# Two order edges in a state-space scan: where the addition to Y and the product dt*x stand in VectorE's queue

## The chip, the cores and the metric

The kernel runs on one core of one Trainium2 chip. The metric is device microseconds of one execution; the figure compared is the median of several runs. In what follows PE is TensorE, DVE is VectorE, ACT is ScalarE, POOL is GpSimd and SP is SyncE, which here only issues DMAs.

## The reference, cut to what matters

Four layers are applied in turn to a float32 image batch of shape (8, 64, 64, 64). The first three (attention over a whole image, two blocks of window attention, a dynamic filter with a 1x9 convolution) run beside the change. The change lies in the fourth, which contains a selective scan in four directions. Per image there are K = 4 directions, DI = 128 channels, L = 4096 positions and N = 16 states:

```python
dts = softplus(einsum(dts, dtproj_w) + dtproj_b)          # dt per channel and position
A = -exp(A_logs)
h = h * exp(dt * A) + dt * B * u                           # for each of the 16 states
y = sum over the states of h * C                           # for each channel and position
out_y = y + D * u
...
y = out_y[:, 0] + inv[:, 0] + wh + invwh                   # the four directions are added
```

## The kernel before, in words

The eight images are taken as four pairs. While the fourth layer's scans of one pair run, the same instruction streams carry other work: the end of the pair before (`back`) and the first layers of the pair after (`front`: attention, window attention, filter, scan inputs). The function `scans` hands out both in small pieces, and a scheduler that builds the program then fixes one order for each engine. It places each instruction by its own estimates of when its inputs are ready, so an instruction may stand ahead of others that were handed out before it. The order edge `net.behind(a, b)` (L445) tells that scheduler to place `a` after `b`; it adds no semaphore.

The scans of a pair are cut into 64 units: two images, four directions in the order 1, 3, 0, 2, and eight pieces of 512 positions (`TD`). A unit has eight steps of two states each. With step number i counted through the pair, one turn of the loop in `scans` does this:

- `fetch` has SP issue the transfers that spread the B row of step i+3 and the C row of step i+2 over the partitions (L1759, 256 KB each, tiles `B` and `C`, four buffers each).
- `products` has POOL form v = B * (dt*x) for step i+2 (L1767, 128x1024, eight buffers).
- `step` does for each of its two states an exponential on ACT into a PSUM bank (L1789, tile `dad`), the scan on DVE (L1792), the copy of the scan's last column on ACT (L1800, tile `carry`), and the product with C on POOL or DVE (L1803, L1806).
- `sums` has PE add the products into the PSUM tile `yd` (L1818, four matmuls a step). `yd` has one buffer; a unit's first sum can start only when the unit before has been read out of it.
- Where i is 2 modulo 8, `gather` is called for the unit before: DVE adds `yd` to the accumulator `Y` (L1831 for the first direction, with D*x; L1833 for the next two; L1836 for the last, into the tile `xs`, which SP then stores).
- After steps 0, 1 and 2 of a unit come `load`, `inputs` and `spread` of the next unit. `inputs` computes dt: PE (L1730) into a PSUM bank, tile `pdd`, then ACT exponential, logarithm and copy (L1732, L1735, L1736); PE and ACT then make the B and C rows (L1738, L1740) and SP stores them (L1742). `spread` has DVE form dt*x from that bank (L1748; it and dt go into the tile `du1`, which has one buffer) and SP issue the two transfers that spread dt and dt*x from there over the partitions (L1752, 512 KB each, tile `du`).

`pdd`, `pbc` and `dad` share three PSUM banks (tag `da`); in the last pair the exponentials also use the three banks of the other work. A bank with dt in it is freed when dt*x has been formed.

In what follows the 16 scans of a unit are counted 0 to 15; step 2 has scans 4 and 5.

Of the kernel before, what the change touches and what calls it, by code (L numbers as in the profile page):

```python
# [11 lines left out]
ALU = mybir.AluOpType  # L12
# [226 lines left out]
class _Net:  # L239
    def __init__(self, ctx, tc, x, packs, layout, out):  # L240
        self.tc, self.nc = tc, tc.nc
        self.x, self.out = x, out
        nc = self.nc
        self.const = ctx.enter_context(tc.tile_pool(name="const", bufs=1))
        self.dram = ctx.enter_context(tc.tile_pool(name="rows", bufs=2, space=bass.MemoryType.DRAM))
        self.packs, self.layout, self.w = packs, layout, {}
        self.load(self.const, (0, 1))
        with tc.tile_pool(name="temp", bufs=1) as temp:
            self.load(temp, (2,))
            self.prepare()  # L250
# [910 lines left out]
class _Direct:  # L1161
# [8 lines left out]
    def __init__(self, net, ctx):  # L1170
        self.net, self.tc, self.nc, self.w = net, net.tc, net.nc, net.w
        tc = self.tc
        self.dram = ctx.enter_context(tc.tile_pool(name="mem", bufs=2, space=bass.MemoryType.DRAM))
        self.slabs = ctx.enter_context(tc.tile_pool(name="slabs", bufs=3))
        self.ps = ctx.enter_context(tc.tile_pool(name="ps_scan", bufs=3, space=PSUM))
        self.pf = ctx.enter_context(tc.tile_pool(name="ps_front", bufs=3, space=PSUM))
        self.kept = {}
        self.turn = -1
        self.dense = 0

    def begin(self, ctx):


        tc = self.tc
        with tc.tile_pool(name="slabs0", bufs=3) as slabs, tc.tile_pool(name="w00", bufs=2) as pool:
            ahead = _Apart(self, slabs, pool).first(1)
            front = first = done = 0
            for cost in self.front(0):
                front += cost
                if cost == 0:  # L1190
                    first = front
                while first and done < AHEAD * (front - first):
                    done += next(ahead, front)
            self.run(ahead)
        one = ctx.enter_context(tc.tile_pool(name="scan1", bufs=1))
        self.Y = one.tile([P, L], F32, name="Y", tag="Y")
        self.carries = one.tile([P, NST], F32, name="carry", tag="carry")
        self.sw = ctx.enter_context(tc.tile_pool(name="scan", bufs=2))
        return front, first
# [544 lines left out]
    def spread(self, u):  # L1744

        nc, one = self.nc, u["one"]
        du = u["du"] = self.sw.tile([P, GRP, 2, TD], F32, name="du", tag="du")
        nc.vector.tensor_tensor(one[:, 1], u["pd"], u["x"], ALU.mult)  # L1748
        m = P // GRP
        for g in range(GRP):  # L1750
            src = one[m * g : m * g + m].rearrange("c q t -> c (q t)").unsqueeze(1).to_broadcast([m, GRP, 2 * TD])
            nc.sync.dma_start(du[:, g].rearrange("p q t -> p (q t)"), src)  # L1752
# [16 lines left out]
    def step(self, i, st):  # L1769

        nc, w, net = self.nc, self.w, self.net
        wk, ps = self.sw, self.ps
        u = self.units[i // 8]
        k, c, at, CC, v = u["k"], u["c"], u["at"], st["C"], st["v"]


        n0 = 2 * (i % 8)
        own = 1 + (i % 4 == 3) if u["image"] >= B - 2 else i % 2 + self.dense
        rev = k >= 2

        def along(t):
            return t[:, ::-1] if rev else t

        h = wk.tile([P, 2 - i % 2, TD], F32, name="hd", tag=f"h{i % 2}", bufs=2)
        hs = []
        for j in range(2):
            n = n0 + j
            da = self.bank("dad", (P, TD), "da")
            nc.scalar.activation(da, u["du"][:, j, 0], AF.Exp, scale=net.As[:, k, n : n + 1])  # L1789
            first = 0.0 if at == 0 else self.carries[:, n : n + 1]  # L1790
            to = da if j >= 2 - own else h[:, j]
            nc.vector.tensor_tensor_scan(along(to), along(da), along(v[:, j]), first, ALU.mult, ALU.add)  # L1792
            hs.append(to)
            if at < NTD - 1 and (own or j):
                ends = h[:, :, 0] if rev else h[:, :, TD - 1]
                cs = self.carries[:, n0 : n0 + 2]
                if own:
                    ends = to[:, 0:1] if rev else to[:, TD - 1 : TD]
                    cs = self.carries[:, n : n + 1]
                nc.scalar.activation(cs, ends, AF.Copy)  # L1800

        if own == 0:
            st["w"] = nc.gpsimd.tensor_tensor(v, h, self.twice(CC), ALU.mult)  # L1803
        for j in range(2 if own else 0):
            engine = nc.vector if j >= 2 - own else nc.gpsimd
            m = engine.tensor_tensor(v[:, j], hs[j], CC, ALU.mult)  # L1806
            st.setdefault("w", m)
# [16 lines left out]
    def gather(self, u):  # L1824

        nc, net, k, c = self.nc, self.net, u["k"], u["c"]
        y = u["y"]
        yd = net.part(self.Y, k, c)
        yp = y.rearrange("p (a b) -> p a b", b=64)
        if u["nth"] == 0:  # L1830
            nc.vector.scalar_tensor_tensor(yd, self.img(u["x"]), net.dsum, yp, ALU.mult, ALU.add)  # L1831
        elif u["nth"] < 3:
            nc.vector.tensor_tensor(yd, yd, yp, ALU.add)  # L1833
        else:
            o = u["x"]
            nc.vector.tensor_tensor(self.img(o), yd, yp, ALU.add)  # L1836
            nc.sync.dma_start(u["out"][:, c * TD : (c + 1) * TD], o)


# [152 lines left out]
```

## Time and profile before

| | |
|---|---|
| median of 3 runs | 12877.57 us (12873.15 to 12906.72) |
| the profiled execution, its own time | 12896.13 us |
| its span in the trace | 12894.0 us |
| mean granted TensorE clock | 0.817 |
| busy: PE, DVE, POOL, ACT | 9714.9, 8570.4, 7760.9, 7066.2 us |
| DVE: L1831, L1833, L1836 (256 in all) | 70.5, 125.3, 43.7 us |
| DVE: L1748 (256) | 174.0 us |
| DVE: the scans L1792 (4096) | 2712.4 + 1782.6 + 363.5 + 248.9 us |

Busy time is the time in which an engine executes. Idle time ahead of an instruction is charged to the instruction that ended it. The first 2200 us of the span hold the first layers of pair 0, with the first layer of pair 1 beside them, and no scans; then the four pairs of scans run one after the other to the end.

### The profile page before, as it was taken

Reading aid. Unit: us, or ns where it says so; the run is one execution under the profiler, and the core shown is the slowest. Engines: PE = TensorE matmul, PEld = TensorE weight load, DVE = VectorE, ACT = ScalarE, POOL = GpSimd, SP = SyncE. Lnnn points to the kernel's source line nnn. Section 1 sums busy time; section 2 is a strip of 40 time slices with the busy share of each in tenths; the row PEclk is TensorE's granted clock in tenths of the full one; section 3 lists DMA queues with packets and bytes.
Section 4 is the critical chain, followed back from the end, with each engine's and each line's share of the span. In section 5 each row is a group of like instructions: output and inputs, shape, how many; then the busy total and the mean of one; then the engine's idle time right before and its main releaser. Section 6 shows DMA issues by size and latency. Waiting matters only on the chain. (4 is left out here: it accounts for less than half of the span.)

```text
span 12894.0 us, 141975 instructions
## 1 busy us (share of the span) xinstructions
PE 9714.9 (75%) x46358; PEld 3162.6 (25%) x46358; DVE 8570.4 (66%) x10061; ACT 7066.2 (55%) x15577; POOL 7760.9 (60%) x3875
## 2 busy tenths in 40 slices
PE   9999985788786558988888556997898655555556
PEld 2243421333221112224332111222342101111111
DVE  0121245788878785467776778358776778998888
ACT  5556523565646655655654645665654645455444
POOL 0000001999899883457765795347775698877774
PEclk9999976787787678988888667998888767777667
DMA  0000002555555552334443564234443456556553
GB/s 25 1 1 1 1 13 87 160 165 158 159 162 167 177 162 84 98 119 128 139 124 108 168 182 129 70 104 135 136 123 105 142 179 192 172 167 187 173 172 125
DMA packets 779985, 1579.99 MB, mean 123 GB/s; under 512 B 89312, under 2 KB 89440, under 8 KB 778208
## 3 DMA queue, kind: packets, MB, share of 16 engines
q1 hardware_dynamic: 755040, 1514.49, 38.5%
q10 hardware_dynamic: 24192, 56.32, 1.1%
q8 instruction: 367, 6.01, 0.2%
q14 instruction: 386, 3.16, 0.1%
HBM read 1199.26 MB, written 102.76 MB: 101 GB/s over the span
## 5 line engine op out<-in xcount | busy, mean ns | idle before, releaser
L1767 POOL TENSOR_TENSOR vd<-B,du 128x1024 f32<-128x1024 f32 x2048 | 4816.6, 2370 | 3728.7 <-DMA B<-rows 2391.2
L1818 PE MATMUL yd<-vd,pack 128*64 128x512 f32 x8192 | 3042.7, 782 | 1327.0 <-POOL vd L1806 648.1
L1789 ACT ACTIVATE dad<-du,As 128x512 f32<-128x512 f32 x4096 | 2734.4, 681 | 1236.0 <-DVE hd L1792 568.7
L1792 DVE TENSOR_TENSOR_SCAN hd<-dad,carry,vd 128x512 f32<-128x512 f32 x2166 | 2712.4, 1270 | 510.2 <-ACT dad L1789 295.7
L1803 POOL TENSOR_TENSOR vd<-hd,C 128x1024 f32<-128x1024 f32 x658 | 1557.8, 2367 | 648.4 <-DVE hd L1792 372.5
L1806 POOL TENSOR_TENSOR vd<-hd,C 128x512 f32<-128x512 f32 x1154 | 1484.4, 1291 | 614.9 <-DVE hd L1792 599.3
L1792 DVE TENSOR_TENSOR_SCAN dad<-dad,carry,vd 128x512 f32<-128x512 f32 x1418 | 1782.6, 1273 | 87.4 <-ACT dad L1789 87.2
L1320 ACT ACTIVATE e<-s 128x512 f32<-128x512 f32 x2048 | 1202.9, 592 | 835.4 <-PE s L1314 833.8
L1818 PEld LDWEIGHTS yd<-vd,pack 128*64 128x64 f32 x8192 | 657.3, 166 | 3329.1 <-POOL vd L1806 1120.2
L1314 PE MATMUL s<-X 64*128 64x512 f32 x4096 | 1302.2, 650 | 43.0 <-ACT e L1320 35.2
L1806 DVE TENSOR_TENSOR vd<-dad,C 128x512 f32<-128x512 f32 x1626 | 1081.4, 677 | 289.7 <-ACT carry L1800 269.0
L1306 PE MATMUL po<-e,VT 128*64 128x512 f32 x4096 | 1204.8, 625 | 7.4 <-ACT e L1320 7.2
L1800 ACT ACTIVATE carry<-hd 128x1 f32<-128x1 f32 (+1 forms) x1586 | 313.9, 201 | 741.1 <-DVE hd L1792 731.1
L1730 PE MATMUL pdd<-xs,xdt 128*128 128x512 f32 x512 | 406.0, 886 | 375.0 <-DVE hd L1792 168.7
L1472 PE MATMUL w_av<-vals,wide 64*64 64x9 f32 x16384 | 624.7, 213 | 36.4 <-ACT wide L1462 36.1
L1472 PEld LDWEIGHTS w_av<-vals,wide 64*64 64x64 f32 x16384 | 597.2, 155 | 216.7 <-issue 90.6
L1457 DVE TENSOR_TENSOR wide<-w_s,bias 128x512 f32<-128x512 f32 x512 | 329.3, 681 | 394.0 <-PE w_s L1444 389.5
L1800 ACT ACTIVATE carry<-dad 128x1 f32<-128x1 f32 x1422 | 239.0, 168 | 630.4 <-DVE dad L1792 626.3
L1314 PEld LDWEIGHTS s<-X 64*128 64x128 f32 x4096 | 355.4, 187 | 912.6 <-issue 794.3
L1329 DVE COPY att<-po 128x512 f32<-128x512 f32 x32 | 21.9, 686 | 755.9 <-PE po L1306 755.9
L1247 PE MATMUL pv<-n_sq,pack 128*128 128x512 f32 x576 | 355.8, 702 | 183.5 <-ACT n_sq L1245 175.8
L1833 DVE TENSOR_TENSOR Y<-Y,yd 128x512 f32<-128x512 f32 x128 | 125.3, 979 | 519.9 <-PE yd L1818 519.9
(246 smaller groups left out, 11236.7 us busy)
## 6 DMA issues: line engine op xcount, KB each, us to landing
B<-rows SPq DMA_DIRECT2D x2048, 256.0 KB, 3.6
C<-rows SPq DMA_DIRECT2D x2048, 256.0 KB, 3.4
du<-du SPq DMA_DIRECT2D x512, 512.0 KB, 6.1
xs<-xt SPq DMA_DIRECT2D x128, 256.0 KB, 3.7
xs<-xc SPq DMA_DIRECT2D x128, 256.0 KB, 3.8
xc<-xcv ACTq DMA_DIRECT2D x64, 256.0 KB, 2.1
zs<-z ACTq DMA_DIRECT2D x64, 256.0 KB, 3.5
xt<-XT ACTq DMA_DIRECT2D x32, 512.0 KB, 5.3
```

The costliest lines, as they stand in the source:

```text
L1306: nc.tensor.matmul(po[half[im]], lhsT=VT[:, t, half[im]], rhs=es[im], start=(t == 0), stop=(t == 31))
L1314: nc.tensor.matmul(ss[im], lhsT=at(half[im], t), rhs=X[half[im], jc * CH : (jc + 1) * CH], start=True, stop=True)
L1320: nc.scalar.activation(e, ss[im], AF.Exp, scale=C**-0.5, accum_out=parts[:, im, t, jc : jc + 1])
L1472: nc.tensor.matmul(self.av[half[im], x % 4 + j, h, :], lhsT=es[h // 4][half[im], j, h % 4, :], rhs=V[half[im], x + j, h, :], start=True, s ...
L1730: nc.tensor.matmul(pd, lhsT=net.xdt[:, k, :], rhs=x, start=True, stop=True)
L1767: self.nc.gpsimd.tensor_tensor(v, self.twice(st["B"]), self.units[i // 8]["du"][:, :, 1], ALU.mult)
L1789: nc.scalar.activation(da, u["du"][:, j, 0], AF.Exp, scale=net.As[:, k, n : n + 1])
L1792: nc.vector.tensor_tensor_scan(along(to), along(da), along(v[:, j]), first, ALU.mult, ALU.add)
L1800: nc.scalar.activation(cs, ends, AF.Copy)
L1803: st["w"] = nc.gpsimd.tensor_tensor(v, h, self.twice(CC), ALU.mult)
L1806: m = engine.tensor_tensor(v[:, j], hs[j], CC, ALU.mult)
L1818: m = nc.tensor.matmul(u["y"][self.HALF[j]], lhsT=w["fold"], rhs=st["v"][:, j], start=(i % 8 == 0), stop=(i % 8 == 7))
```

## The change

The class keeps the DVE scan that was issued last in `self.scanned`. Two order edges are added: the addition to `Y` in `gather`, and the product dt*x in `spread`, are placed behind that scan. Both are called after step 2 of a unit, so the scan is the second one of step 2, scan 5. The first dt*x of a pair stands behind the last scan of the pair before, and only the first of the whole run has no scan to stand behind. No instruction is added or taken away, and no semaphore is changed by hand; the scheduler builds all five queues anew.

```diff
     def spread(self, u):
...
-        nc.vector.tensor_tensor(one[:, 1], u["pd"], u["x"], ALU.mult)
+        m = nc.vector.tensor_tensor(one[:, 1], u["pd"], u["x"], ALU.mult)
+        if self.scanned is not None:
+            self.net.behind(m, self.scanned)
...
     def step(self, i, st):
...
-            nc.vector.tensor_tensor_scan(along(to), along(da), along(v[:, j]), first, ALU.mult, ALU.add)
+            self.scanned = nc.vector.tensor_tensor_scan(
+                along(to), along(da), along(v[:, j]), first, ALU.mult, ALU.add
+            )
...
     def gather(self, u):
...
+        o = u["x"]
         if u["nth"] == 0:
-            nc.vector.scalar_tensor_tensor(yd, self.img(u["x"]), net.dsum, yp, ALU.mult, ALU.add)
+            m = nc.vector.scalar_tensor_tensor(yd, self.img(o), net.dsum, yp, ALU.mult, ALU.add)
         elif u["nth"] < 3:
-            nc.vector.tensor_tensor(yd, yd, yp, ALU.add)
+            m = nc.vector.tensor_tensor(yd, yd, yp, ALU.add)
         else:
-            o = u["x"]
-            nc.vector.tensor_tensor(self.img(o), yd, yp, ALU.add)
+            m = nc.vector.tensor_tensor(self.img(o), yd, yp, ALU.add)
+        net.behind(m, self.scanned)
+        if u["nth"] == 3:
             nc.sync.dma_start(u["out"][:, c * TD : (c + 1) * TD], o)
```

More of the change, by code (lines that the diff above doesn't have):

```diff
@@ L1179, in __init__ @@
         self.dense = 0
+        self.scanned = None
     def begin(self, ctx):
```

## The prediction

> **What bounds the kernel now.** I read the busy shares by stretch first, then DVE's waits, then the timeline around the two moved instructions, then POOL's waits.
>
> By stretch (us of the stretch, then busy us of PE, PE loads, DVE, ACT, POOL, granted clock, DMA):
>
> ```profile
> 2200.00:4750.00 2550.00, 1867.27 (x9443) 623.99 (x9444) 2050.27 (x2253) 1492.94 (x2948) 2308.47 (x1126) 0.78 0.54 166
> 4750.00:5750.00 1000.00, 851.06 (x2926) 238.38 (x2924) 584.20 (x660) 597.11 (x1647) 432.27 (x214) 0.90 0.33 98
> 10900.00:12790.00 1890.00, 1060.84 (x2278) 240.11 (x2278) 1654.49 (x1783) 947.02 (x2129) 1469.25 (x785) 0.73 0.57 175
> ```
>
> The limit changes. In the first stretch of scans POOL is busy 91%, DVE 80%. From 4750 to 5750 (and 7800 to 8700) the other work is attention: PE sets the pace, DVE and POOL idle. At the end DVE is busy 88%. Between these no engine is over 85%, and units follow chains of waits.
>
> DVE's waits (total us, times, longest), and who waited for dt*x:
>
> ```profile
> DVE Y L1833 <- PE yd L1818: 519.9, 74, 51.6
> DVE hd L1792 <- ACT dad L1789: 334.3, 178, 8.2
> DVE du L1748 <- ACT du L1736: 78.0, 54, 6.3
> ...
> ACT dad L1789: 33.8, 51
> ```
>
> The additions to Y wait 519.9 + 43.3 (L1831) + 51.8 (L1836) = 615 us for PE's sums, dt*x waits 79 us. These are what the change could win. The second line warns: the scans that would go ahead have waits of their own, for exponentials. How the two go together (DVE and ACT of one unit; start, duration):
>
> ```profile
> 3413.02 1.11 DVE L1831 SCALAR_TENSOR_TENSOR Y<-xs,dsum,yd 128x512 f32<-128x512 f32 x1 [1.79 <-PE yd L1818]
> ...
> 3414.95 0.60 ACT L1736 ACTIVATE du<-pdd 128x512 f32<-128x512 f32 x1
> ...
> 3415.70 0.68 DVE L1748 TENSOR_TENSOR du<-pdd,xs 128x512 f32<-128x512 f32 x1
> 3415.92 1.28 ACT L1789 ACTIVATE dad<-du,As 128x512 f32<-128x512 f32 x2
> ...
> 3416.69 2.46 DVE L1792 TENSOR_TENSOR_SCAN hd<-dad,carry,vd 128x512 f32<-128x512 f32 x2 [0.31 <-ACT dad L1789]
> ```
>
> DVE waits 1.79 us for the sums, adds, forms dt*x, and then still waits 0.31 us: the exponentials of scans 4 and 5 stand in ACT's queue behind the computation of dt (L1736 and before). Had the scans stood first, DVE would have waited for them until 3416.69 all the same.
>
> Last, the transfers that dt*x starts, late in the last pair, and POOL's total for them:
>
> ```profile
> du<-du SPq DMA_DIRECT2D x512, 512.0 KB, 6.1
> POOL vd L1767 <- DMA du<-du: 231.3, 47, 8.8
> ...
> 12061.33 1.20 SPq L1752 DMA_DIRECT2D du<-du  x2
> ...
> 12066.60 1.30 ACT L1789 ACTIVATE dad<-du,As 128x512 f32<-128x512 f32 x2 [7.04 <-DMA du<-du]
> ...
> 12068.02 0.69 DVE L1806 TENSOR_TENSOR vd<-dad,C 128x512 f32<-128x512 f32 x1 [5.76 <-ACT carry L1800]
> ...
> 12068.95 2.35 POOL L1767 TENSOR_TENSOR vd<-B,du 128x1024 f32<-128x1024 f32 x1 [6.49 <-DMA du<-du]
> ```
>
> Where these transfers are issued late, ACT, DVE and POOL all stop for 6 to 7 us.
>
> **The sum's base.** The profiled execution took 12896.1 us (span 12894.0 and 2.1 around it), 18.6 above the median of 12877.6. I work out a difference and add it to the median.
>
> **What moves.** In the built order, 197 of the 256 additions stood after scans 0 to 3 and ahead of scan 4; now 244 stand behind scan 5. Of the dt*x, 90 stood ahead of scan 4, 43 ahead of scan 5 and 118 behind it; now 245 are behind. All the queues are made anew: on SP the two `du` transfers move from on average 1.2 B or C transfers ahead of the next unit's first to 0.1 behind it; POOL's order around a unit's first product is unchanged in 227 of 256 units.
>
> **Won: waits of the additions.** About 406 of the 615 us lie in the two attention stretches, where PE's queue is the limit: worth nothing. Of the other 209 us little can be filled: of 100 additions ahead of scan 4 that waited over 0.3 us, scan 4 still lacked its exponential or product at the end of the wait in 90. Laying the passed scans into the waits at the time their inputs were ready fills 30 us over the whole run. I take -30; the bound is -209. For dt*x the bound is its 79 us and the 34 us in which exponentials wait for its bank; since it waits for the ACT chain that those exponentials stand behind, I take -10.
>
> A page speaks against the change here: the Trainium skill (Perfetto Trace Analysis, Identifying the Most-Contended Engine) has one work on the gaps of the engine with the highest occupancy of a regime. From 2200 to 4750 us that is POOL and not DVE, so by it DVE's waits of that stretch would be worth 0; by DVE's list alone they would count in full.
>
> **Lost: work that filled waits.** The moved work is 70.5 + 125.3 + 43.7 + 174.0 = 413.5 us (L1831, L1833, L1836, L1748). Counted unit by unit, 244 us of it ran while the scan behind it still lacked its inputs: free work, 27 us of it in the attention stretches. Behind scan 5 DVE does it when scans 6 and 7 are mostly ready (its waits before those two are 45 us in all). The cost lies between 0, where DVE has time later, and 217 us. In the last stretch, where DVE is the fullest engine, it is 43 us, counted in full; of the other 174 us I take 12. Together +55.
>
> **Lost: `du` on SP's queue.** There are 16 B and C transfers in a unit of (12790 - 2200) / 256 = 41 us, so one place is 2.6 us; the 1.3 places make 3.4 us. Today the first product of the next unit starts a median of 2.1 us after `du` has landed (under 0.5 us in 73 units, under 3.5 in 173). Putting each unit's pair behind the B or C transfer that now precedes it, at that transfer's time in the trace, raises POOL's waits at the first product by 717 us: 239 in the first stretch, 86 in the attention stretches, 161 in the last pair's, the remaining 231 in the stretches without a full engine. That is an upper bound, since those B and C transfers get out earlier by the pair's 1.2 us.
>
> How much reaches the end? In pair 0's units where `du` already stood at place 0 or later (8 units), POOL idled 3.7 us at the first product and a unit took 38.2 us; elsewhere 1.5 and 37.2: 1.0 of 2.3 us. In the mixed stretches late units are not longer (45.3 against 46.8 us): none. In the last pair, where nothing runs beside, four successive units with `du` at -3, -1, 0 and +1 took 26.5, 28.9, 30.8 and 32.4 us: all. So 0.44 x 239 = 105, 0 for attention, 0.1 x 231 = 23, 0.5 x 161 = 80, together 208; as the 717 is an upper bound I take about half, +110, between 0 and 400.
>
> The Trainium skill (DMA: Bandwidth & Descriptors, Anatomy of one DMA — SWDGE (gpsimd) path) fits a DMA by 2.0 us plus its bytes by 436 GB/s, for another queue than SP: 3.2 us for 512 KB. The row above measures 6.1; with the page's 2.9 us less, most of the lateness would be hidden and this term would be about 0.
>
> **Others, taken at 0.** The bank with dt is held two scans longer in 90 units and one in 43; an exponential (0.68 us) with two banks left still fits under a scan (1.27 us). Were it not so, 223 scans by 0.68 us is 152; if the exponentials now get another bank, -34. `yd` is freed two scans (2.5 us) later; PE waits for it 89 us in 25 places today, and the next sums are ordered behind step 3's product, so 0; at most 25 x 2.5 = 63. On SP the load L1722 waits for L1831 11 times (43 us): at most 28.
>
> Sum: -30 - 10 + 55 + 110 = +125 us: 13002.6, say 13003.
>
> **The rivals.** *Faster.* DVE's waits were what held the scans back. If the scheduler now puts the exponentials of scans 4 and 5 ahead of the dt chain, DVE and POOL get on by up to 209 + 79 us; with 70% of that on the path (-200) and half the `du` term (+55) it would be 12733. It decides where the exponentials move up. Against it: in the built order the copy of dt stands after four of the unit's exponentials in 118 units, 120 before. *Same.* Units follow POOL, PE or the other work, and both sides cancel: 12878. *Much slower.* Half of the `du` bound outside attention reaches the end, 0.5 x 631 = 315, plus 55: 13248. It decides if the late product makes the B and C transfers behind it late too. *The edges do nothing*: excluded by the new order.
>
> **How the numbers follow.** Forecast 0.53, faster 0.20, same 0.15, much slower 0.12. A measurement of this kernel can tell about 0.3% (39 us) from no change. Faster by more is 0.20, within 0.15, slower 0.65. The range leaves about a tenth out on each side: 12790, part of the way to the faster case, to 13230, just below the much slower one.
>
> **What would show it.** Right: the waits of L1833 shrink but those of scan 4 for its exponential grow by about as much; POOL's wait for `du` rises from 231 us to 400 or more; the first stretch and the last pair get longer, the attention stretches do not. Wrong: waits for `yd` vanish without new ones at scans 4 and 5, or the `du` waits stay at 231 us.

## The result, and the profile after

| | before | after |
|---|---|---|
| median of 4 runs | 12875.36 us | 13171.33 us |
| lowest to highest | 12854.2 to 12906.72 | 13165.49 to 13186.78 |
| the profiled execution, its own time (span) | 12896.13 (12894.0) | 13175.76 (13174.0) |

The two edges make the kernel slower by 296 us: ratio 1.0231, 95% interval 1.0211 to 1.025. The forecast had 125 us. The mean granted TensorE clock was 0.806 to 0.810 in the runs after; in 76 runs of the kernel before, beside the experiments, it was 0.815 to 0.822. Whether the lower clock adds to the loss or only goes with it was not tested; in the attention stretch shown below, where PE sets the pace, it is 0.90 before and 0.91 after.

DVE's waits after, total us, times, longest:

```profile
DVE hd L1795 <- ACT dad L1792: 988.9, 256, 28.6
...
DVE Y L1837 <- PE yd L1823: 1.8, 2, 1.3
...
DVE du L1749 <- ACT du L1737: 4.4, 1, 4.4
```

The additions and dt*x now wait 8 us in all. The wait of the scans into the tile `hd` for their exponentials went from 334.3 to 988.9 us. The largest of the four groups of scans before and after (count, busy us, mean ns, then DVE's idle time just ahead of them and what ended it):

```profile
L1792 DVE TENSOR_TENSOR_SCAN hd<-dad,carry,vd 128x512 f32<-128x512 f32 x2166 | 2712.4, 1270 | 510.2 <-ACT dad L1789 295.7 <-POOL vd L1767 182.8 <-POOL vd L1803 20.3
L1795 DVE TENSOR_TENSOR_SCAN hd<-dad,carry,vd 128x512 f32<-128x512 f32 x2166 | 2719.2, 1269 | 1109.7 <-ACT dad L1792 878.8 <-POOL vd L1770 204.5 <-POOL vd L1808 14.4
```

Counted as all idle time of DVE just ahead of these instructions, additions, dt*x and all scans had 615 + 80 + 701 = 1396 us before and have 4 + 4 + 1387 = 1395 us after. The waits were not removed; they changed names.

The same unit as in the timeline shown for before, now after (start, duration; DVE and ACT):

```profile
3443.34 0.66 ACT L1733 ACTIVATE pdd<-pdd,pack 128x512 f32<-128x512 f32 x1
...
3445.01 0.66 ACT L1792 ACTIVATE dad<-du,As 128x512 f32<-128x512 f32 x1
3445.62 0.57 ACT L1737 ACTIVATE du<-pdd 128x512 f32<-128x512 f32 x1
3445.78 2.46 DVE L1795 TENSOR_TENSOR_SCAN hd<-dad,carry,vd 128x512 f32<-128x512 f32 x2 [0.31 <-ACT dad L1792]
...
3448.15 1.07 DVE L1837 SCALAR_TENSOR_TENSOR Y<-xs,dsum,yd 128x512 f32<-128x512 f32 x1
...
3449.07 0.68 DVE L1749 TENSOR_TENSOR du<-pdd,xs 128x512 f32<-128x512 f32 x1
3449.66 1.27 DVE L1795 TENSOR_TENSOR_SCAN hd<-dad,carry,vd 128x512 f32<-128x512 f32 x1
```

Scans 4 and 5 wait 0.31 us for the same exponential as before, which stands in ACT's queue behind the start of the dt chain (L1733). Before, the addition and dt*x had been done by then. Now they come behind scan 5 and keep scan 6 back by 1.5 us (3448.15 to 3449.66).

POOL's wait for `du`, in its list of waits:

```profile
POOL vd L1770 <- DMA du<-du: 438.5, 99, 8.3
```

And the transfers in the page's DMA part (KB each, median us from issue to landing):

```profile
du<-du SPq DMA_DIRECT2D x512, 512.0 KB, 6.3
```

POOL waited for `du` 231.3 us in 47 places before and 438.5 us in 99 now; a transfer takes about as long as before (6.3 against 6.1 us), it starts later.

By stretch, the two with an engine at its limit and the last pair (the same distance from the end as the row shown of before; busy us of PE, PE loads, DVE, ACT, POOL, then clock, DMA):

```profile
2200.00:4750.00 2550.00, 1833.70 (x9330) 622.65 (x9328) 1980.64 (x2188) 1452.66 (x2847) 2230.75 (x1090) 0.77 0.53 160
4750.00:5750.00 1000.00, 849.68 (x2783) 233.94 (x2782) 578.06 (x635) 603.61 (x1651) 436.18 (x214) 0.91 0.33 101
11180.00:13070.00 1890.00, 1014.09 (x2186) 234.35 (x2182) 1630.23 (x1741) 913.71 (x2061) 1446.41 (x772) 0.71 0.56 171
```

In the first, POOL falls from 2308 to 2231 us and makes 1090 instructions instead of 1126; the attention stretch is as before; at the end all engines are a little emptier. By units of scans (counted 0 to 255 from their starts in the traces), with POOL's wait for `du` at the units' first products. This wait is counted until `du` has landed, whatever POOL waited for last, and without the very first unit; the list above counts only the waits that `du` ended, so its totals are smaller (231.3 us against 390 before).

| units | length before | after | POOL's `du` wait before | after |
|---|---|---|---|---|
| 0 to 73 (first stretch) | 2853 | 2940 | 56 | 155 |
| 74 to 86 (attention) | 702 | 710 | 10 | 15 |
| 87 to 112 | 1212 | 1263 | 22 | 58 |
| 113 to 149 (its second half attention) | 1811 | 1821 | 35 | 72 |
| 150 to 191 | 1873 | 1971 | 35 | 93 |
| 192 to 255 (last pair) | 2242 | 2278 | 232 | 281 |

The last row runs to the end of the span. Such a table comes from one execution of each kernel, and the times of the kernel before spread over 53 us, so 10 or 20 us in one cell may be chance.

### The profile page after: what moved, and what is told of

It reads as the page before. It is cut to its first block, busy times and chain, and to the rows that moved or that the text cites. A ratio compares the mean times of both kernels' runs of the same rounds, so it can differ in the third digit from the quotient of the medians.

```text
span 13174.0 us, 141999 instructions
## 1 busy us (share of the span) xinstructions
PE 9804.2 (74%) x46358; PEld 3212.5 (24%) x46358; DVE 8674.7 (66%) x10061; ACT 7076.7 (54%) x15584; POOL 7766.0 (59%) x3875
## 5 line engine op out<-in xcount | busy, mean ns | idle before, releaser
L1463 ACT ACTIVATE wide<-wide 128x512 f32<-128x512 f32 x512 | 309.8, 625 | 308.3 <-DVE wide L1458 179.7
```

## The experiments

The times of a run stand against runs of the kernel before on the same chip. The theories: the work put behind scan 5 costs, because it no longer fills waits (W); the later `du` costs (L); the later reading of `yd` costs.

**The edges one by one.** Only `net.behind(m, self.scanned)` in `gather`, then only the one in `spread`.

> Only the addition to Y has its edge; dt*x is free as before. In the built order 245 additions stand behind scan 5, and the du transfers stand on average 0.96 places ahead of the next unit's first B or C transfer (before 1.22 ahead, changed kernel 0.13 behind). Theory A, lost filling: the addition's 240 us of work leave waits that they filled and DVE then waits for the exponential of scan 4 with nothing to do; the time rises by 100 to 200 us over 12875. Theory B, late du: the place of du hardly moves, so within 60 us of 12875, and POOL's wait for du stays near 231 us.

> Only dt*x has its edge; the addition to Y is free. 245 dt*x stand behind scan 5, the additions stand where they stood (201 ahead of scan 4); du stands on average 0.38 places ahead of the next unit's first transfer. Theory A: about half of the 174 us of dt*x stood ahead of scan 4 or 5, so the loss is at most 90 us. Theory B: du has moved 0.84 of the 1.35 places that it moves in the changed kernel, so about 0.62 of the 296 us, 180 us, and POOL's wait for du 350 us or more.

| run | time | difference | ratio | POOL for `du` (waits list) |
|---|---|---|---|---|
| addition's edge alone | 13053.54 | +174 | 1.0138 (1.0121 to 1.0155) | 241.1 |
| dt*x's edge alone | 13006.85 | +127 | 1.0109 (1.0092 to 1.0126) | 384.0 |

The differences add up to 301 us, the whole change. With the addition's edge alone POOL waits for `du` no longer than before (231.3), and DVE's list has the same swap:

```profile
DVE hd L1793 <- ACT dad L1790: 818.5, 218, 28.6
```

So 174 us come with hardly a later `du`. The 127 us of the other edge lie between the two expectations (at most 90, about 180) and have both causes in them.

**What of the addition costs: its place, or its work?** The addition on one of the eight rows of its tile (the rest of the sums left out), without an edge and behind scan 5. That is 64 of 512 columns, not 8 as the expectations have it, and 65 and 61 us of work in place of 240 (profile rows of the three additions):

```diff
-            m = nc.vector.tensor_tensor(yd, yd, yp, ALU.add)
+            m = nc.vector.tensor_tensor(yd[:, 0:1], yd[:, 0:1], yp[:, 0:1], ALU.add)
...
+        net.behind(m, self.scanned)          # in the second run only
```

> No edge, and the addition to Y works on 8 of its 512 columns (the rest of the sum over directions is left out), so it keeps its waits and its place (197 ahead of scan 4) but has next to no work; Y is cleared once. For comparison with narrow_behind. Theory A (the addition's work filled a wait, and costs nothing where it stands): at most 60 us below 12879. Theory C (place alone matters): the same; it is the next run that tells.

> The same narrow addition, with the addition's edge: 245 behind scan 5; du stands on average 1.34 places ahead, as in narrow_free (1.33). Theory A, the lost filling is the addition's own work, done later on DVE: with next to no work left, within 50 us of narrow_free. Theory C, it is the later place: yd is freed two scans later, PE's next sums, POOL's buffers and the scans follow: 120 us or more above narrow_free, as gather_only (13054) is 174 above before.

12850.41 us without an edge (ratio 0.9983, 0.9973 to 0.9992) and 12854.63 us behind scan 5 (0.9988, 0.9975 to 1.0001). DVE's waits of the second:

```profile
DVE hd L1794 <- ACT dad L1791: 815.8, 199, 28.6
```

This run has the full 816 us wait of the scans, and `yd` is read as late as after the change, and the two together cost 4 us. What costs is the work: the 174 us of it taken out where it stood are worth only 27 us (12877.89 to 12850.41), while behind scan 5 the 174 us between 235 and 61 cost 13053.5 - 12854.6 = 199 us.

**Between scan 4 and scan 5.** The addition's edge alone, to the first scan of step 2:

```diff
+            if j == 0:
+                self.scanned = m             # the scan just issued
```

> The edge on the addition alone, tied to scan 4 and not to scan 5: in the list it stands behind the fifth scan of a unit in 133 units and behind the sixth in 117. If the loss is the wait before scan 4, which the addition filled and now doesn't: nearly all of the 174 us of the addition's edge to scan 5 stays, 130 to 180 us slower than before, and VectorE's wait for scan 4's exponential above 700 us. If the price grows with how far the addition is put back: half of it, 60 to 110 us.

12884.47 us, +8 (ratio 1.0006, 0.9994 to 1.0017). Both expectations fell: the scans' wait is the same as with the edge to scan 5, 812.1 us, and in sum nothing is lost.

```profile
DVE hd L1793 <- ACT dad L1790: 812.1, 194, 28.6
```

In 133 units the built order now has the addition between scans 4 and 5. These took 58 us less than before; with the edge to scan 5 the same units took 87 us more. The 145 us between exceed the 119 us that their additions last. In the 117 units where the scheduler set it behind scan 5 all the same, the two runs differ by 13 us: these units are 58 us longer than before in this run and 72 us longer in the other. So the sum of +8 us has a gain and a loss of 58 us in it, and the line runs at scan 5: ahead of it the addition costs nothing, behind it its own time and a little more.

**Other work at the same places.** To see whether any work behind scan 5 costs, one more DVE instruction a unit, needed by nobody, held between two scans by edges on both sides; the rest as before:

```diff
+            if i % 8 == 2 and j == 0:        # ahead of scan 4; the other run: i % 8 == 3 and j == 0, behind scan 5
+                self.extra = nc.vector.tensor_reduce(net.spare, u["x"], AX.X, ALU.add)
```

> One more VectorE instruction in each unit, a sum over one 128x512 tile (some 0.6 us, 150 us in all), its order fixed between scan 3 and scan 4 of its own unit. It depends on nothing late. If VectorE's waits ahead of scan 4 hide work put there: at most 50 us slower than before. If they don't: 100 to 150 us.

> The same extra instruction, its order fixed between scan 5 and scan 6. If work behind scan 5 costs its own time and more, whatever it is (the addition there cost 174 us for 240 us of work): 100 to 180 us slower than before, and the 174 us of dt*x put there explain its edge's 127 us. If it isn't the work but what waits for its result: within 50 us of the run with the instruction ahead of scan 4, and dt*x's edge costs by the later du.

The instruction's row in each run:

```profile
L1795 DVE TENSOR_REDUCE dsum<-xs 128x1 f32<-128x512 f32 x256 | 170.7, 667 | 0.0
```

```profile
L1795 DVE TENSOR_REDUCE dsum<-xs 128x1 f32<-128x512 f32 x256 | 171.5, 670 | 0.0
```

Ahead of scan 4 its 171 us cost 54 us (12942.10; ratio 1.0049, 1.0032 to 1.0067), slightly above the 50 expected; behind scan 5 they cost 166 us (13054.28; 1.0133, 1.0116 to 1.015). POOL's wait for `du` is 248.2 us there (231.3 before), so `du` is hardly later. Theory W holds, with its price: the work's own time.

**`du` early again.** Both edges, and the first B transfer of a unit placed behind that unit's `du` pair on SP:

```diff
+        if i % 8 == 0 and s == 0 and sent is not None:
+            self.net.behind(d, sent)         # sent: the du transfer; d: the B transfer
```

> Both edges as in the changed kernel, and on SP the B transfer of a unit's first step is placed behind that unit's du transfers: du stands on average 1.27 places ahead, as before the change, while 244 additions and 245 dt*x stand behind scan 5. Theory A: the loss stays, 150 to 300 us over 12875. Theory B: the loss goes, within 80 us of 12875, and POOL's wait for du is back near 231 us.

13147.04 us, +268 (ratio 1.0206, 1.0189 to 1.0223). It did not part the theories. POOL no longer waits for `du`, but for the B rows that SP now holds back until dt*x is there:

```profile
POOL vd L1767 <- DMA B<-rows: 2391.2, 61, 2182.0
POOL vd L1773 <- DMA B<-rows: 2761.3, 147, 2174.3
```

The first line is that of the kernel before; some 2180 us in each are the wait for the very first row. Here the lateness only changed its owner.

**`du` late, and nothing else.** No DVE edge; the two `du` transfers handed out two steps later on SP: in all units, in two of three, in two of five (in the others one step, which moves them by 0.1 to 0.3 places).

```diff
+            if i >= 0 and i % 8 == 4 and i // 8 + 1 < len(self.units):
+                self.send(self.units[i // 8 + 1])     # the loop of L1752, taken out of spread
```

> No edge on DVE. The du transfers alone are handed out two steps later and placed behind the B and C transfers of that turn: on average 0.77 places behind the next unit's first transfer, more than in the changed kernel (0.13), while additions and dt*x stand as before (198 and 95 ahead of scan 4). Theory A: at most 60 us over 12875. Theory B: more than the whole loss, 250 to 450 us over 12875, with POOL's wait for du above 438 us.

> No DVE edge, and the additions and dt*x where they stand before; in two of three units the du transfers are handed out two steps later, in the third one step later. In SP's list they then stand 0.2 places behind the next unit's first B or C transfer on average, spread about as in the changed kernel (0.13 behind; before 1.2 ahead, two steps later in all units 0.8 behind). The lateness of du in the changed kernel without the moved work, then. If the work put behind scan 5 is what costs, by the narrow dt*x (27 us left of 127) and the run with du's place given back (28 us won): 20 to 80 us slower than before, although POOL's wait for du is 400 us or more. If the lateness costs most of what its POOL waits grow by, as in the run two steps later: 150 to 250 us slower.

> No DVE edge; the du transfers handed out two steps later in two of five units and one step later in the others, which puts them on average 0.37 places ahead of the next unit's first B or C transfer (with the edge on dt*x alone 0.38 ahead, before 1.2). If the lateness is what the edge on dt*x costs: 90 to 170 us slower than before, with a wait of POOL at the first product near that run's. If it is dt*x's work behind scan 5: 10 to 60 us.

| run | `du` against the next unit's first transfer | POOL's `du` wait at first products | difference | ratio |
|---|---|---|---|---|
| before | 1.2 places ahead | 390 | | |
| two of five late | 0.37 ahead | 569 | +112 | 1.0094 (1.0073 to 1.0114) |
| two of three late | 0.20 behind | 691 | +242 | 1.0186 (1.0169 to 1.0203) |
| all late | 0.77 behind | 803 | +296 | 1.0231 (1.0214 to 1.0248) |
| dt*x's edge alone | 0.38 ahead | 605 | +127 | 1.0109 |
| the change | 0.13 behind | 674 | +296 | 1.0231 |

A place in this table, in the prediction and in the expectations is the number of B and C transfers ahead of a unit's `du`, less 16 for each unit before it. Since SP issues a unit's first B transfers ahead of the last C transfers of the unit before, this is not quite the distance to the unit's own first transfer: by the traces `du` stood on average 0.3 places behind that one before and stands 1.9 behind it after the change. The order of the runs is much the same by both counts.

Of the growth of POOL's wait, 112 of 179, 242 of 301 and 296 of 413 us reach the end: 0.63 to 0.80. The run with two of three late, which has the change's lateness and none of its moved work, loses 242 us where theory W expected 20 to 80. So L holds too. For dt*x's edge, the lateness alone would give 112 of the 127 us. But some 130 dt*x of 0.68 us moved behind scan 5 as well; by the extra instruction's price that is an estimated 85 us more. The two together exceed 127 us, so how the loss of this edge divides between them is not shown.

**Narrow dt*x.** Dt*x on 8 of its columns (the rest left out; the tile `du1` is then one fixed tile, cleared once), without an edge and behind scan 5:

```diff
-        m = nc.vector.tensor_tensor(one[:, 1], u["pd"], u["x"], ALU.mult)
+        m = nc.vector.tensor_tensor(one[:, 1, 0:8], u["pd"][:, 0:8], u["x"][:, 0:8], ALU.mult)
```

> No edge; dt*x on 8 of its 512 columns (the rest of dt*x left out), which takes some 170 us of work out of VectorE's list where it stands before. If that work lies in VectorE's waits there, as the addition's did (240 us of work left out, 27 us won): 10 to 50 us faster than before. If it lies on the path: 120 to 180 us faster.

> The same narrow dt*x, placed behind scan 5. The run with the edge on dt*x alone lost 127 us. If those are the unfilled wait before scan 4, with dt*x's own 170 us put behind the scans: this one within 30 us of the narrow dt*x without an edge. If they are the later du (its transfers again issued about half a step later than without the edge, and POOL's first product waits for them): 80 to 150 us slower than the narrow one without an edge, and POOL's wait for du above 330 us.

12905.03 and 12932.37 us: 28 and 56 us slower than before (ratios 1.002, 1.001 to 1.003, and 1.0038, 1.0025 to 1.0051). The first is a miss: with 134 us less work (174 to 40) it should not be slower, and I did not find why; the scheduler built all the queues anew around the shorter instruction. Their difference of 27 us is 0.17 of the 159 us by which POOL's `du` wait grows (328 to 487). That fits neither the 0.63 to 0.80 of the runs above nor, with the work gone, anything of W. It remains unexplained, and so the price of a late `du` is known for those three runs only.

**The other way round.** Scan 4 placed behind the addition and dt*x, the edges turned about; then dt computed one step earlier with scan 4 behind the addition alone:

```diff
+            if i % 8 == 2 and j == 0:
+                for m in (self.first, self.added):    # dt*x and the addition
+                    if m is not None:
+                        net.behind(self.scanned, m)
```

> The opposite edges: scan 4 is placed behind the addition and behind dt*x, which are handed out before step 2. 242 additions and 197 dt*x stand ahead of scan 4, none or few behind scan 5; du stands on average 1.83 places ahead (before 1.22). Late du has a price by du_late_only of 296 us for 1.99 places; if that line holds on this side, 0.61 places give -90 us: 12790. If earlier du no longer matters because it already lands in time in most units: 12850 to 12900. If scan 4 now has to wait for dt in the units in which dt*x stood behind scan 5 (118): 12950 or more.

> The loading of the next unit's input, the computing of dt and dt*x are handed out one step earlier, and scan 4 is placed behind the addition: 113 dt*x stand after 2 scans, 53 after 3 and 80 after 4 (before: 90 after 4, 118 after 6); du stands on average 2.37 places ahead. By the line of du_late_only 1.15 places would give -170 us: 12710. If POOL is held by other waits once du lands in time: -30 to -80 us. If the earlier dt chain on ACT holds back the exponentials of scans 2 and 3 instead: 12900 or more.

The first took 12843.19 us (ratio 0.9973, 0.9963 to 0.9983), 35 us faster than before and the fastest version that computes everything; it lies between the expected 12790 and 12850. In the profiled executions its last pair is 107 us shorter than before, the rest some 58 us longer. POOL's wait for `du` nearly goes:

```profile
POOL vd L1770 <- DMA du<-du: 30.3, 16, 5.1
```

The second took 12871.46 us (0.9995, 0.9984 to 1.0005), no difference, and in none of the three expected ranges: the scans then wait for the dt chain, which now stands ahead of their exponentials (DVE's waits):

```profile
DVE dad L1797 <- ACT dad L1794: 594.9, 92, 53.3
DVE hd L1797 <- ACT dad L1794: 263.9, 163, 10.6
...
DVE Y L1845 <- PE yd L1829: 47.9, 39, 8.6
```

## Why the prediction was right or wrong

The sign, the two costs named and the signs to look for were right. 13171 lies in the range, but the forecast of 13003 had less than half of the loss. Two terms of the sum were too small, and both in the same step: in the stretches where no engine was read as full they were priced at next to nothing.

**Won, -40.** Right that the waits can't be had: 1396 us of idle time became 1395. A gain of 30 us for the addition cannot be told apart in the runs.

**"Lost: work that filled waits", +55: failed.** The additions alone, the edge's own gains taken in, lost 174 us against -30 and a part of 55. The bounds 0 to 217 held the size; the value taken in them did not. I priced the work in full only in the last stretch, 43 us, and took 12 of 174 elsewhere, since no engine was full there and DVE idles later in the unit. By stretch, three runs lost (their unit lengths less those of before):

| units | 0-73 | 74-86 | 87-112 | 113-149 | 150-191 | 192-255 |
|---|---|---|---|---|---|---|
| addition's edge alone | +41 | +4 | +1 | +48 | +53 | +13 |
| extra instruction behind scan 5 | +37 | +11 | 0 | +24 | +32 | +55 |
| two of three `du` late | +88 | +3 | +25 | +54 | +52 | +3 |

The extra instruction shows the price of plain work: 57 of its 70 us come out in units 87 to 191, where the prediction gave next to nothing, and 55 of 43 in the last pair, where it gave the full time. Ahead of scan 4 the same instruction costs 5 us in units 87 to 191. So what was read there as slack was none behind scan 5. That DVE's waits there lie in the chain that sets the pace is the likely reason; no chain was followed to show it. Nor do all of these stretches lack a full engine: POOL is busy 89 and 95% in the two 250 us from 7250 to 7750. In the last pair the addition's edge costs only 13 us, because the addition was on the path there already: with the narrow addition at its old place the last pair is 35 us shorter. So the 43 us counted in full there were too many for a move, and the 12 elsewhere far too few.

**"Lost: `du` on SP's queue", +110: failed in two of its factors.** The bound of 717 us is far off: the change's places cost POOL 301 us of wait without the edges, and 284 in the change. The halving answered to that. But the share that reaches the end was taken as 0.44, 0, 0.1 and 0.5 for the first stretch, attention, the mixed stretches and the last pair. Measured in the run with two of three late, as length by wait: 88 of 130 in the first (0.68); 132 of 45 + 25 + 60 = 130 in the mixed ones, units 87 to 191 (some attention among them), all of it; 3 of 41 in the last pair. With two of five and with all late the mixed ones have 63 of 88 and 128 of 154, the last pair 17 of 28 and 21 of 76. The wrong factor is 0.1, where 0.7 to 1 was measured: I took it from units of the trace where `du` happened to be late, which were no longer than others. Those were late in company of other work, and probably of different length for other reasons; a delay laid on many units was the test. In the last pair four units in a row had suggested that all of it reaches the end; less reaches it in each of the three runs, and next to nothing in one.

**The sum.** Alone, the moved addition costs 174 and the later `du` 242 us, together 416, but the change costs 296. So 120 us overlap. I think that work behind scan 5 lies in waits that the late `du` makes anyway, but this was not shown.

**Others at 0.** `yd` read later: 4 us in the narrow pair, right. The bank of dt: exponentials wait for dt*x 92.5 us in 109 places, against 33.8 in 51; not tried alone.

**What to see.** The waits of the additions shrank and the scans' grew by as much; POOL's wait for `du` is over 400 us (438.5); the first stretch is 87 and the last pair 36 us longer, attention 8 us. All as listed, but units 87 to 112 and 150 to 191, of which nothing was said, are 149 us longer, half of the loss.

**The rivals.** "Faster" needed exponentials that move up; they did not: in the traces the copy of dt starts after four of the unit's exponentials in 118 units, 120 before. "Same" fell with the 296 us. "Much slower", 13248, put half of 631 us through, by B and C transfers made late. Its number is nearer to 13171 than the forecast is, but by luck: POOL's wait for B rows went from 2391 to 2327 us, and the waits of POOL and DVE for C rows only from 45 to 80.

On the page of the Trainium skill weighed there (Perfetto Trace Analysis, Identifying the Most-Contended Engine), which has one optimize the engine with the highest occupancy first, so that DVE's waits of the first stretch would count 0: their removal was worth nothing, as that has it. But DVE is not free there either: the moved work cost 41 us in a stretch in which POOL is the fullest engine. On the other (DMA: Bandwidth & Descriptors, Anatomy of one DMA — SWDGE (gpsimd) path), 3.2 us for 512 KB: the changed kernel's 6.3 us is the measured one, and a lateness term of 0 is refuted by 242 us.

**Open:** why the addition costs nothing just ahead of scan 5; the narrow dt*x; how dt*x's loss divides; and the overlap.

## What to carry to other kernels

Before removing a wait, find what the next instruction in the same queue waits for: if it is as late, only the wait's name changes, and the work that stood behind the old wait may now stand on the path. In a stretch without a full engine, idle time need not be slack; test by one harmless instruction put at the new place, as here, where 171 us cost 54 us at one place and 166 us two scans later. And of an edge on the producer of a transfer, count the transfer: later `du` transfers alone cost 112 to 296 us here.

## What was not expected of the hardware

One DVE instruction has no fixed length. Two instructions of the other work, side by side, before (count, then ns min/median/max):

```profile
L1858 DVE SCALAR_TENSOR_TENSOR u<-pc,pack,n_sd x64: 718/728/752, 4450.9 to 12791.3; 128x512 f32<-128x512 f32 x64
L1859 DVE SCALAR_TENSOR_TENSOR u<-u,pack,big x64: 725/1434/17091, 4452.1 to 12792.1; 128x512 f32<-128x512 f32 x64
```

And the second after:

```profile
L1866 DVE SCALAR_TENSOR_TENSOR u<-u,pack,big x64: 725/1810/13155, 4519.7 to 13071.9; 128x512 f32<-128x512 f32 x64
```

The first reads PSUM (`pc`) and SBUF, the second SBUF twice. The first keeps its length though 57 of its 64 instances run beside POOL. The second lasts 0.72 to 0.75 us without POOL and up to 17 us with it: over its 64 instances length and overlap with POOL's work go together with a correlation of 0.99 before and 1.0 after. The longest, from 4628.2 to 4645.3 us, lasted until POOL's unbroken row of instructions ended at 4644.7 us: through eight of them, and not only the one that was running. In all it takes 118 us before and 184 us after. The Trainium skill (GPSIMD Engine Reference, Specifications) names such a contention: POOL shares its SBUF interfaces with DVE, and instructions of DVE with two SBUF inputs meet it. The rows agree. So of DVE's 104 us more of busy time (8570 to 8675), 66 are this one instruction meeting POOL more often. They are not what the 296 us are made of: it takes as long with the addition's edge to scan 4 (169 us) and with the narrow addition behind scan 5 (179 us), and those runs lose 8 us and nothing.
